# A compressed interaction network: V1 and V0 as packed matmuls of 32 by 64, and another order in the head

## The chip, the cores and the metric

The kernel runs on one core of one Trainium2 chip. A core has TensorE (PE, matmuls from SBUF into PSUM), VectorE (DVE), ScalarE (ACT), GpSimd (POOL) and SyncE (SP, which here only issues DMAs); each works through its own queue in order and waits for others by semaphores. PEld is TensorE's loading of weights. The metric is the time of one execution on the device, in microseconds; lower is better.

## The reference: what is computed

For a batch of B = 1024 with F = 64 fields and E = 16 elements, all in fp32, with `x` of shape (1024, 64, 16):

```python
x0, h, xs = x, x, []
for i in range(3):                                   # W[i]: (128, 64 * 64), b[i]: (128,)
    z = einsum('bfe,bge->bfge', x0, h)               # products of all pairs of rows
    y = einsum('oc,bce->boe', W[i], z.reshape(B, 64 * 64, E)) + b[i][None, :, None]
    if i < 2: x_i, h = y[:, :64], y[:, 64:]          # half goes out, half goes on
    else:     x_i = y
    xs.append(x_i)
out = sum(concatenate(xs, axis=1), axis=2) @ fc_w.T + fc_b      # (1024, 1)
```

## The kernel before

**The algebra.** Only a weighted sum of the outputs is wanted. So the last layer's weights are first contracted with fc (v2t, 64 numbers for each half), and then with the second layer's (a matrix M, written to DRAM as `md` and read back mirrored as `ms`). The outputs of layers 0 and 1 that go out directly come to quadratic forms in x (V0) and in x and h1 (V1), where V0 and V1 are 64x64 matrices: W0 and W1 weighed with fc.

**The chunks.** N = 512 columns (32 batch rows by 16 elements) make one chunk; there are 32 of them. A chunk's x is loaded twice: `xa` (128 rows by 4 tiles; x at shifted rows) and `xb` (4 further shifts), 1 MB each. `product` (line 219) multiplies them on VectorE, four instructions of 128x2048 for a chunk, into 16 tiles z of 128x512. `contract` (line 256) multiplies the 16 tiles by `w_all` on TensorE and adds up in one PSUM tile `acc`: 64 columns of weights make h1, 64 others make q. Of the last group's first tile 32 rows are squares x*x, written by ScalarE (line 228).

**The packed block.** For every 4 chunks `contract_shared` (line 265) adds what is left. V1 times x goes into `acc` (line 274), V0 times x into a PSUM tile `y` for two chunks (line 278): 64x64 matmuls whose operand `xx` holds one chunk's 64 rows of x in the upper half of the partitions and the next chunk's in the lower half. V1 lies twice, one below the other, in `v1w`; V0 lies twice on the diagonal of the 128x128 tile `bd`. The squares of rows 0 to 31 of four chunks lie in the four row groups of one tile `sq`; they are multiplied as 32x64 matmuls (line 284). `xx` and `sq` are filled by ScalarE from `xa`: one copy of 64x512 (line 243) and one square of 32x512 (line 234) for a chunk.

**The head.** Four chunks, HEAD = [2, 3, 0, 1], are worked on before M is known. For the first two, `xb` isn't loaded but shifted out of `xa` by matmuls with a shift matrix (`shift_pair`, line 180, into PSUM tiles xp). `half_contract` (line 291) contracts only h1 for them; `keep_h1` saves it in SBUF. Between the four, TensorE makes v2t (line 411) and M (line 435, tiles pm); ScalarE copies pm to `m_sb` (line 445); six DMAs write it to `md` (lines 460 to 470, on the queues of SP and ScalarE), more read it back (lines 497 and 503), and VectorE adds it up as weights (`q_weights`, line 533). Then `head_q` (line 314) contracts q for the kept chunks, and the normal chunks follow in the order 4, 5, 6, 7, 2, 3, 8, 9, ... (line 618), chunks 2 and 3 standing for both kept pairs' turns. V1 is weighed after the products of chunk 4 (lines 576 to 582), V0 after those of chunk 5 (line 586 on).

**What sets the order.** The schedule is written out by hand: on each engine instructions run in the order in which the program issues them. DMAs on SP's queue are issued in that order too, so one that waits for its buffer holds up those behind it. Tiles come from pools with a fixed number of buffers (`bufs`); a tile that is asked for anew waits for the last use of the one whose place it takes.

**Start.** Six matmuls with `bd` (set to zero by GpSimd; `keep_clock(6)`, line 107) run before x has landed, another one after the first shifts, and then two matmuls for the constant `cst` (line 198).

## Time and profile before

| | |
|---|---|
| median of 3 runs | 486.74 us (486.42 to 490.46) |
| the profiled execution | 486.68 us, its span 484.9 us |
| instructions in the trace | 4057 |
| TensorE busy | 479.8 us (99%) |
| VectorE busy | 370.4 us (76%) |
| ScalarE busy | 93.8 us (19%) |
| GpSimd busy | 17.3 us (4%) |
| SP's DMA queue | 77.05 MB, 41.4% of 16 engines' span |
| `contract`, line 260 | 928 records, 387.3 us |
| V1, line 274 / V0, line 278 | 66 / 64 records, 15.5 us each |
| squares, line 284 | 132 records, 8.9 us and more (two forms) |
| ScalarE's copies to xx, line 243 | 32, 0.613 us each |
| ScalarE's squares to sq, line 234 | 32, 0.628 us each |

The span runs from the first to the last instruction in the profile; the execution's own time is 1.8 us longer. "Busy" counts the time in which at least one instruction of an engine ran, so matmuls that run side by side in different parts of the array count once. The chain that ended last is followed back from the end, at each step to what released it. In a timeline's line stand the start in us, the length in us, engine, line of the kernel, operation, output and inputs, shape and count, and in brackets the idle time before it with what ended it. Every fp32 matmul leaves two records.

### The profile page before, as it was taken

How to read it: one execution, taken by the hardware profiler on the slowest of the kernel's cores; microseconds unless marked ns; L12 is line 12 of the kernel's file. 1: busy time of each engine (PE TensorE's matmuls, PEld its weight loads, DVE VectorE, ACT ScalarE, POOL GpSimd, SP SyncE). 2: the span in 40 equal slices, each digit the busy share in tenths (PEclk: the TensorE clock that was granted, in tenths of full speed). 3: DMA queues.
4: the chain of work that ended last, by engine and by line, in shares of the span. 5: the costliest groups of instructions: out<-in, count | busy, mean ns of one | idle time of the engine just before them, and what ended most of it. 6: DMA issues, size and time to landing. Idle time of an engine off the chain costs nothing.

```text
span 484.9 us, 4057 instructions
## 1 busy us (share of the span) xinstructions
PE 479.8 (99%) x1672; PEld 215.7 (44%) x1672; DVE 370.4 (76%) x234; ACT 93.8 (19%) x165; POOL 17.3 (4%) x15
## 2 busy tenths in 40 slices
PE   9999999999999999999999999999999999999996
PEld 4564344443344344444444344443444434444465
DVE  5984799998899988898887686767878676771312
ACT  4244012021212030312221012212022121020001
POOL 5350000000000000000000000000000000000000
PEclk9999999999999999999999999999999999999999
DMA  8986984441743453547343344433344430000000
GB/s 334 412 266 181 427 349 174 173 173 64 307 182 142 173 207 140 194 174 279 113 187 120 148 174 173 161 128 105 126 173 173 170 145 32 0 1 0 0 2 0
DMA packets 14392, 78.59 MB, mean 162 GB/s; under 512 B 3778, under 2 KB 4450, under 8 KB 5478
## 3 DMA queue, kind: packets, MB, share of 16 engines
q1 hardware_dynamic: 13266, 77.05, 41.4%
q10 hardware_dynamic: 1108, 1.28, 1.0%
q8 instruction: 13, 0.21, 0.2%
q14 instruction: 5, 0.04, 0.0%
HBM read 76.69 MB, written 1.64 MB: 162 GB/s over the span
## 4 chain that ended last, share of the span: by engine, by line
PE 97%; DVE 1%; ACT 1%; SPq 1%; issue 1%; DMA 0%; POOL 0%; DVEq 0%; POOLq 0%
PE acc L260 80%; PE acc L314 6%; PE acc L296 4%; PE acc L274 3%; PE acc L284 2%; PE xp L184 1%; PE misc L105 1%; SPq L465 0%; DVE z L223 0%; ACT m_sb L445 0%; PE pv L411 0%; DMA md<-m_sb 0%; PE pm L435 0%; PE y L278 0%; PE po L604 0%
## 5 line engine op out<-in xcount | busy, mean ns | idle before, releaser
L260 PE MATMUL acc<-z,w_all 128*128 128x512 f32 (+1 forms) x928 | 387.3, 578 | 0.0
L223 DVE TENSOR_TENSOR z<-xa,xb 128x2048 f32<-128x2048 f32 x125 | 280.7, 2286 | 41.4 <-PE acc L260 34.8
L260 PEld LDWEIGHTS acc<-z,w_all 128*128 128x128 f32 x928 | 175.5, 190 | 211.3 <-issue 205.8
L228 ACT ACTIVATE z<-xa 32x512 f32<-32x512 f32 x34 | 21.3, 626 | 322.7 <-DVE z L223 318.1
L336 DVE SCALAR_TENSOR_TENSOR uu<-acc,vs,q 64x512 f32<-64x512 f32 (+1 forms) x29 | 21.2, 731 | 57.7 <-ACT q L330 57.5
L296 PE MATMUL acc<-z,w_all 128*64 128x256 f32 x256 | 28.9, 381 | 0.2 <-DVE z L223 0.2
L314 PE MATMUL acc<-z,w_all 128*64 128x512 f32 x128 | 27.9, 593 | 0.0
L330 ACT COPY q<-acc 64x512 f32<-64x512 f32 (+1 forms) x33 | 18.7, 567 | 37.4 <-PE acc L260 21.2
L223 DVE TENSOR_TENSOR z<-xa,xp 128x2048 f32<-128x2048 f32 (+2 forms) x10 | 18.1, 1856 | 7.2 <-PE xp L184 6.0
L296 PEld LDWEIGHTS acc<-z,w_all 128*64 128x64 f32 x256 | 18.0, 137 | 11.0 <-issue 1.3
L234 ACT ACTIVATE sq<-xa 32x512 f32<-32x512 f32 x32 | 20.1, 628 | 3.4 <-DMA xa<-in_xra 2.7
L345 DVE TENSOR_REDUCE acc<-uu 128x64 f32<-128x1024 f32 (+3 forms) x19 | 20.3, 1073 | 0.3
L243 ACT COPY xx<-xa 64x512 f32<-64x512 f32 x32 | 19.6, 613 | 0.3
L314 PEld LDWEIGHTS acc<-z,w_all 128*64 128x64 f32 x128 | 9.1, 137 | 18.0 <-issue 17.9
L278 PE MATMUL y<-xx,bd 64*64 64x512 f32 x64 | 15.5, 603 | 0.0
L274 PE MATMUL acc<-xx,v1w 64*64 64x512 f32 (+1 forms) x66 | 15.5, 588 | 0.0
L341 DVE SCALAR_TENSOR_TENSOR uu<-y,cx,xx 128x512 f32<-128x512 f32 x16 | 11.3, 746 | 0.2
L223 POOL TENSOR_TENSOR z<-xa,xb_gps 128x2048 f32<-128x2048 f32 x2 | 9.1, 4568 | 4.7 <-ACT xb_gps L361 4.4
L284 PE MATMUL acc<-sq,w_sq 32*64 32x512 f32 (+1 forms) x132 | 8.9, 599 | 0.0
L274 PEld LDWEIGHTS acc<-xx,v1w 64*64 64x64 f32 x66 | 4.1, 132 | 10.6 <-issue 10.3
L223 POOL TENSOR_TENSOR z<-xa,xb 128x2048 f32<-128x2048 f32 x1 | 6.6, 6570 | 13.3 <-DVE z L223 13.3
L184 PE MATMUL xp<-xa,shift 64*64 64x512 f32 x32 | 5.5, 786 | 0.1
(57 smaller groups left out, 60.0 us busy)
## 6 DMA issues: line engine op xcount, KB each, us to landing
xa<-in_xra SPq DMA_DIRECT2D x32, 1024.0 KB, 5.0
xb<-in_xrb SPq DMA_DIRECT2D x31, 1024.0 KB, 7.1
w<-in_w2t SPq DMA_DIRECT2D x2, 1024.0 KB, 10.9
xa<-in_xra SPq DMA_DIRECT2D x2, 768.0 KB, 7.9
w1s<-in_w1h SPq DMA_DIRECT2D x1, 1024.0 KB
w1x<-in_wx SPq DMA_DIRECT2D x1, 1024.0 KB
w0x<-in_wx SPq DMA_DIRECT2D x1, 1024.0 KB, 8.3
w0t<-in_w0r SPq DMA_DIRECT2D x1, 768.0 KB
```

The costliest lines, as they stand in the source:

```text
L223: engine.tensor_tensor(zs[c, j][:, at, :], xas[c][:, at, :], xbs[c][j].unsqueeze(1).to_broadcast([128, last - first, N]), ALU.mult,)
L228: nc.scalar.activation(zs[c, j][SQ, 0, :], xas[c][SQ, 0, :], AF.Square)
L234: nc.scalar.activation(sqs[c // 4][at], xas[c][0:32, 0, :], AF.Square)
L243: nc.scalar.copy(xxs[c // 2][to], xas[c][to, 0, :])
L260: nc.tensor.matmul(acc_c, w_all[:, t, w_cols(c)], zs[c, j][:, i, cols], start=(t == 0 and c % 4 < 2), stop=(t == NT - NI and c % 4 >= 2),)
L274: nc.tensor.matmul(acc_c[q], v1w[rows], xxs[k][rows, cols], start=(c not in ends), stop=False,)
L284: nc.tensor.matmul(acc_c[halves[n]], w_sq[at, w_cols(c)][:, 64 * n : 64 * n + 64], sqs[first // 4][at, cols], start=h and (first == 0 or c ...
L296: nc.tensor.matmul(accs[c][halves[n]], w_all[:, t, 0:64], zs[c, j][:, i, n * H2 : (n + 1) * H2], start=(t == 0), stop=(j == last and i == ...
L314: nc.tensor.matmul(accs[c][halves[1 - c % 2]], w_all[:, t, 64:128], zs[c, j][:, i, :], start=(t == 0), stop=False,)
L330: nc.scalar.copy(q[h, cols], acc_c[64 - h.start : 128 - h.start])
L336: nc.vector.scalar_tensor_tensor(uu[:, cols], acc_c[h], bh1[h], q[h, cols], ALU.add, ALU.mult)
L345: nc.vector.tensor_reduce(acc[rows, of, k, half], uus[k][rows, of, E * half.start : E * half.stop].rearrange("p k (b e) -> p k b e", e=E), ...
```

## The change

Five things are changed.

1. **V1 and V0 in 32x64.** `load_shared` (new) loads x for four chunks into `xr`: 128 rows, chunk n's rows 0 to 31 (part 0) and 32 to 63 (part 1) in row group n. `v1w` and `v0w` hold V1 and V0 by row group and part. Each of the four chunks has for each part one V1 and one V0 matmul of 32x64, so 16 in place of 8.
2. **x by DMA.** `load_shared` also loads `xx` (two DMAs of 256 KB, as `xr` has), and one ScalarE instruction squares 128x512 into `sq`. The function `last_tile` with its copies and squares is gone, for the head's chunks too. `load_shared(n)` is issued after chunk n's own load, for n divisible by four; for chunks 0 to 3 ahead of chunk 8's products.
3. **The weights' copies.** `to_groups` copies V1 and V0 in 32x32 pieces, 16 each, where there were 4 copies of 64x32 each.
4. **The start.** The first matmuls take the zeros that the program always has, seven of 128x128 and one of 128x64; `bd` and the later `keep_clock(1)` are gone. The constant's matmuls stand behind the first two tiles of chunk c0's contraction.
5. **The head's order.** Products of c0 on GpSimd and one on VectorE are cut in two; the second pair of c1's shifts comes after `half_contract(c0, 1)`; `half_contract(c1, 0)` comes after v2t; the last x of c2 is copied into PSUM; the third DMA that writes `md` goes from ScalarE's queue to SP's; the copies of c3's x, with cx behind them, come before `keep_h1(c1)`; GpSimd's product of c3 is issued before c2's contraction and contracted second.

The diff, cut to its core (smaller const tiles now share `res` and `shift`):

```diff
-    keep_clock(6)
+    zeros = nc.const_aps.tensor(0.0, [128, 128])
+    for n in (128,) * 7 + (64,):
+        nc.tensor.matmul(misc[:, 0:n], zeros, zeros[:, 0:n], start=True, stop=True)
...
+    def load_shared(first):
+        xr = xrs[first] = sp.tile([128, 2, N], F32, tag="xr", name=f"xr_{first}")
+        for h in range(2):
+            nc.sync.dma_start(
+                out=xr[:, h, :],
+                in_=bass.AP(
+                    tensor=xra.tensor, offset=(first * XR + 32 * h) * N,
+                    ap=[[XR * N, 4], [N, 32], [1, N]],
+                ),
+            )
+        for k in (first // 2, first // 2 + 1):
+            xxs[k] = sp.tile([128, N], F32, tag="xx", name=f"xx_{k}", bufs=4)
+            nc.sync.dma_start(
+                out=xxs[k],
+                in_=bass.AP(
+                    tensor=xra.tensor, offset=2 * k * XR * N, ap=[[XR * N, 2], [N, F], [1, N]]
+                ),
+            )
+        sqs[first] = sp.tile([128, N], F32, tag="sq", name=f"sq_{first}")
+        nc.scalar.activation(sqs[first], xr[:, 0, :], AF.Square)
...
-    keep_clock(1)
-    cst = const_tile("cst", [128, 1])
...
-            for n in range(2):
-                c, rows, q = 2 * k + n, halves[n], halves[1 - n]
+        groups = {c: slice(32 * (c % 4), 32 * (c % 4) + 32) for c in chunks}
+        for m in range(2):
+            for c, at in groups.items():
+                n, xr = c % 2, xrs[first][groups[c], m]
                 for acc_c, cols in pieces(c):
                     nc.tensor.matmul(
-                        acc_c[q], v1w[rows], xxs[k][rows, cols], start=(c not in ends), stop=False,
+                        acc_c[halves[1 - n]], v1w[at, m], xr[:, cols],
+                        start=(m == 0 and c not in ends), stop=False,
+                        tile_position=(at.start, 64 * (1 - n)),
                     )
-            for rows in halves:
-                nc.tensor.matmul(ys[k][rows], bd[rows, rows], xxs[k][rows], start=True, stop=True)
+                nc.tensor.matmul(
+                    ys[c // 2][halves[n]], v0w[at, m], xr, start=(m == 0), stop=(m == 1),
+                    tile_position=(at.start, 64 * n),
+                )
...
-    product(c0, 1, engine=nc.gpsimd)
+    for i in (0, 2):
+        product(c0, 1, i, i + 2, engine=nc.gpsimd)
...
+    half_contract(c0, 0, at=(0, 1))
+
+    cst = const_tile("cst", [128, 1])
...
-    product(c0, 2)
+    product(c0, 2, 0, 2)
     h1_weights(1, w0o[1])
+    product(c0, 2, 2, NI)
...
-    half_contract(c0, 0)
+    half_contract(c0, 0, at=(2, 3))
...
     shift_pair(c1, (0, 3))
+    half_contract(c0, 1)
     shift_pair(c1, (1, 2))
...
-    half_contract(c0, 1, 2, 3, last=3)
+    half_contract(c0, 2, 3, last=3)
...
-    half_contract(c1, 0)
...
-    half_contract(c1, 3, 1)
+    half_contract(c1, 0, 3, 1)
...
+    xb2 = ps.tile([128, N], F32, tag="set", name=f"xp_{c2}_{NJ - 1}")
+    nc.scalar.copy(xb2, xbs[c2][NJ - 1])
+    xbs[c2][NJ - 1] = xb2
...
-    nc.scalar.dma_start(out=m_ap(64, 32, [[row, 32], [1, 32 * F]]), in_=m_rows[64:96])
+    nc.sync.dma_start(out=m_ap(64, 32, [[row, 32], [1, 32 * F]]), in_=m_rows[64:96])
...
-    keep_h1(c1)
-    squares(c2)
-    new_acc(c2, H2)
     for j in (0, 1):
         xb3 = ps.tile([128, N], F32, tag="y", name=f"xp_{c3}_{j}")
         nc.scalar.copy(xb3, xbs[c3][j])
         xbs[c3][j] = xb3
+    nc.scalar.copy(cx, pcx)
+    keep_h1(c1)
+    new_acc(c2, H2)
     for j in range(NJ):
         product(c2, j)
+    product(c3, NJ - 1, engine=nc.gpsimd)
     half_contract(c2, *range(NJ), last=3)
...
-    half_contract(c3, 0, 1, 3, 2, last=2)
+    half_contract(c3, 0, 3, 1, 2, last=2)
...
-    for c in KEPT:
-        last_tile(c)
...
                 load_chunk(n)
-                last_tile(n)
+                if n % 4 == 0:
+                    load_shared(n)
...
+    def to_groups(w, part):
+        for at in range(0, 128, 32):
+            for n in range(2):
+                for m in range(2):
+                    q = 64 * n + 32 * m
+                    nc.vector.tensor_copy(
+                        w[at : at + 32, m, 32 * n : 32 * n + 32], part[q : q + 32]
+                    )
...
                 for n in order[4:6]:
                     load_chunk(n)
-                    last_tile(n)
+                load_shared(0)
```

More of the change, by code (lines that the diff above doesn't have):

```diff
@@ L96, in cin_kernel @@
     nc.scalar.copy(fv2, fc2.to_broadcast([128, 32]))
-    bd = const_tile("bd", [128, 128])
-    nc.gpsimd.memset(bd, 0.0)
+    v0w = const_tile("v0w", [128, 2, F])
+    v1w = const_tile("v1w", [128, 2, F])
     misc = ps.tile([128, N], F32, tag="acc", name="misc", bufs=4)
-    def keep_clock(n):
-        for _ in range(n):
-            nc.tensor.matmul(misc[:, 0:128], bd, bd, start=True, stop=True)
-    keep_clock(6)
+    zeros = nc.const_aps.tensor(0.0, [128, 128])
+    for n in (128,) * 7 + (64,):
+        nc.tensor.matmul(misc[:, 0:n], zeros, zeros[:, 0:n], start=True, stop=True)
     shift = const_tile("shift", [128, 96])
@@ L125, in cin_kernel @@
     w_sq = const_tile("w_sq", [128, 192])
-    v1w = const_tile("v1w", [128, F])
-    xas, xbs, xxs, sqs = {}, {}, {}, {}
+    res = const_tile("res", [128, 128])
+    xas, xbs, xxs, xrs, sqs = {}, {}, {}, {}, {}
     def load_xa(c, at=slice(0, NI)):
@@ L192, in cin_kernel @@
     shift_pair(c0, (2, 3))
-    keep_clock(1)
-    cst = const_tile("cst", [128, 1])
-    for j in range(2):
-        nc.tensor.matmul(
-            misc[:, 0:1], fcol[:, j : j + 1].to_broadcast([128, 128]), bcol[:, j : j + 1],
-            start=(j == 0), stop=(j == 1),
-        )
     acc = const_tile("acc", [128, 2, NCH // 2, CB])
@@ L228, in product @@
             nc.scalar.activation(zs[c, j][SQ, 0, :], xas[c][SQ, 0, :], AF.Square)
-    def squares(c):
-        if c // 4 not in sqs:
-            sqs[c // 4] = xp.tile([128, N], F32, tag="zl", name=f"sq_{c}", bufs=3)
-        at = slice(32 * (c % 4), 32 * (c % 4) + 32)
-        nc.scalar.activation(sqs[c // 4][at], xas[c][0:32, 0, :], AF.Square)
-    def last_tile(c):
-        if c >= FIRST:
-            squares(c)
-        if c % 2 == 0:
-            xxs[c // 2] = sp.tile([128, N], F32, tag="xx", name=f"xx_{c}", bufs=5)
-        to = halves[c % 2]
-        nc.scalar.copy(xxs[c // 2][to], xas[c][to, 0, :])
     def w_cols(c):
@@ L270, in contract_shared @@
             ys[k] = ps.tile([128, N], F32, tag="y", name=f"y_{k}")
-            for n in range(2):
-                c, rows, q = 2 * k + n, halves[n], halves[1 - n]
+        groups = {c: slice(32 * (c % 4), 32 * (c % 4) + 32) for c in chunks}
+        for m in range(2):
+            for c, at in groups.items():
+                n, xr = c % 2, xrs[first][groups[c], m]
                 for acc_c, cols in pieces(c):
                     nc.tensor.matmul(
-                        acc_c[q], v1w[rows], xxs[k][rows, cols], start=(c not in ends), stop=False,
-                    )
-            for rows in halves:
-                nc.tensor.matmul(ys[k][rows], bd[rows, rows], xxs[k][rows], start=True, stop=True)
-        for c in chunks:
-            at = slice(32 * (c % 4), 32 * (c % 4) + 32)
+                        acc_c[halves[1 - n]], v1w[at, m], xr[:, cols],
+                        start=(m == 0 and c not in ends), stop=False,
+                        tile_position=(at.start, 64 * (1 - n)),
+                    )
+                nc.tensor.matmul(
+                    ys[c // 2][halves[n]], v0w[at, m], xr, start=(m == 0), stop=(m == 1),
+                    tile_position=(at.start, 64 * n),
+                )
+        for c, at in groups.items():
             for acc_c, cols in pieces(c):
@@ L285, in contract_shared, with half_contract @@
                         acc_c[halves[n]], w_sq[at, w_cols(c)][:, 64 * n : 64 * n + 64],
-                        sqs[first // 4][at, cols], start=h and (first == 0 or c not in ends),
+                        sqs[first][at, cols], start=h and (first == 0 or c not in ends),
                         stop=(c in ends), tile_position=(at.start, 64 * n),
                     )
-    def half_contract(c, *js, last=None):
+    def half_contract(c, *js, last=None, at=None):
         for j in js:
-            for i in tiles(j):
+            for i in at or tiles(j):
                 t = j * NI + i
@@ L359, in cin_kernel @@
     new_acc(c0, H2)
-    squares(c0)
     nc.scalar.copy(xb_gps[:, 0, :], xbs[c0][1])
     xbs[c0][1] = xb_gps[:, 0, :]
-    product(c0, 1, engine=nc.gpsimd)
+    for i in (0, 2):
+        product(c0, 1, i, i + 2, engine=nc.gpsimd)
     w0p = ps.tile([128, 2, NI, F], F32, tag="set", name="w0p")
@@ L371, in cin_kernel @@
     product(c0, 0, 2, NI)
+    half_contract(c0, 0, at=(0, 1))
+    cst = const_tile("cst", [128, 1])
+    for j in range(2):
+        nc.tensor.matmul(
+            misc[:, 0:1], fcol[:, j : j + 1].to_broadcast([128, 128]), bcol[:, j : j + 1],
+            start=(j == 0), stop=(j == 1),
+        )
     nc.scalar.activation(cst, misc[:, 0:1], AF.Identity, bias=fcb, scale=float(E))
     nc.scalar.copy(w0o[1], w0s[1][:, :, 1, :])
-    product(c0, 2)
+    product(c0, 2, 0, 2)
     h1_weights(1, w0o[1])
+    product(c0, 2, 2, NI)
     for j in (2, 3):
@@ L390, in cin_kernel @@
     xbs[c1][3] = xb_gps[:, 1, :]
-    squares(c1)
     product(c0, 3)
     load_chunk(c3)
-    half_contract(c0, 1, 2, 3, last=3)
+    half_contract(c0, 2, 3, last=3)
     keep_h1(c0)
@@ L401, in cin_kernel @@
     product(c1, NJ - 1, engine=nc.gpsimd)
-    half_contract(c1, 0)
     v2r = flat_tile("v2r")[:, 0:1024].rearrange("p (n c) -> p n c", n=2)
-    v2t = const_tile("v2t", [128, F])
+    v2t = res[:, 0:F]
     for n in range(2):
-        pv = ps.tile([128, 512], F32, tag=("y", "set")[n], name=f"pv2_{n}")
+        pv = ps.tile([128, 512], F32, tag=("set", "y")[n], name=f"pv2_{n}")
         for k in range(4):
@@ L443, in cin_kernel @@
         nc.tensor.matmul(pcx[to], v2t[0:64], bh2, start=True, stop=True)
+    xb2 = ps.tile([128, N], F32, tag="set", name=f"xp_{c2}_{NJ - 1}")
+    nc.scalar.copy(xb2, xbs[c2][NJ - 1])
+    xbs[c2][NJ - 1] = xb2
     for m in (0, 2, 1, 3):
         nc.scalar.copy(m_sb[:, m, :], pms[m])
-    nc.scalar.copy(cx, pcx)
     half_contract(c1, 2, last=2)
@@ L516, in cin_kernel @@
     new_acc(c3, H2)
-    product(c3, NJ - 1, engine=nc.gpsimd)
     for j in range(NJ - 1):
         product(c3, j)
-    squares(c3)
     keep_h1(c2)
-    half_contract(c3, 0, 1, 3, 2, last=2)
+    half_contract(c3, 0, 3, 1, 2, last=2)
     for j in range(1, NJ):
@@ L526, in cin_kernel @@
             read_columns(j, nc.scalar if half and j == 2 else nc.sync, half)
-    dg = const_tile("dg", [128, F])
+    dg = res[:, F:128]
     nc.sync.dma_start(out=dg[SQ], in_=m_ap(32, 32, [[row + F, 32], [1, F]]))
@@ L571, in weigh @@
         nc.vector.tensor_reduce(out, w, AX.X, ALU.add)
+    def to_groups(w, part):
[5 more added lines that the diff above has]
+                        w[at : at + 32, m, 32 * n : 32 * n + 32], part[q : q + 32]
+                    )
     load_products(FIRST)
@@ L577, in cin_kernel @@
     nc.sync.dma_start(out=w1x, in_=wx1)
-    v1h = const_tile("v1h", [128, 32])
+    v1h = shift[:, 0:32]
     weigh(w1x, fcr[:, 64:128], v1h)
-    for to in halves:
-        for n in range(2):
-            nc.vector.tensor_copy(v1w[to, 32 * n : 32 * n + 32], v1h[halves[n]])
+    to_groups(v1w, v1h)
     load_products(FIRST + 1)
@@ L588, in v0_weights @@
         nc.sync.dma_start(out=w0x, in_=wx0)
-        v0h = const_tile("v0h", [128, 32])
+        v0h = shift[:, 32:64]
         weigh(w0x, fcr[:, 0:64], v0h)
-        for to in halves:
-            for n in range(2):
-                cols = slice(to.start + 32 * n, to.start + 32 * n + 32)
-                nc.vector.tensor_copy(bd[to, cols], v0h[halves[n]])
+        to_groups(v0w, v0h)
     NP = NCH // 2
     QP = NP // 4
-    res = const_tile("res", [128, QP, CB])
+    res = res.rearrange("p (k b) -> p k b", b=CB)
     outs = out.rearrange("(k h b) o -> h k (b o)", h=2, b=CB)
```

## The prediction

> **What bounds the kernel now.** I read the page's busy shares first, then the chain that ended last, then the timelines of single engines where the diff touches them.

> ```profile
> PE 479.8 (99%) x1672; PEld 215.7 (44%) x1672; DVE 370.4 (76%) x234; ACT 93.8 (19%) x165; POOL 17.3 (4%) x15
> ...
> PE 97%; DVE 1%; ACT 1%; SPq 1%; issue 1%; DMA 0%; POOL 0%; DVEq 0%; POOLq 0%
> ```

> TensorE works for 479.8 of 484.9 us and carries 97% of the chain. So an edit counts where it shortens or stops TensorE; VectorE counts only where TensorE catches up with it, ScalarE hardly at all. The profiled execution took 486.68 us, 1.8 us more than its span; the median of the runs shown, 486.74, lies 0.06 us off. I add to 486.68. A change under 1% of this (4.9 us) is about what a measurement of this kernel cannot tell from none: its three runs lie between 486.42 and 490.46.

> **The packed block (V1, V0, squares).** It runs 8 times, once for 4 chunks. This is TensorE's timeline of one (columns: start, us, then engine, line, operation, count):

> ```profile
> 217.25 0.65 PE L274 MATMUL acc<-xx,v1w 64*64 64x512 f32 x2
> 217.26 0.65 PE L278 MATMUL y<-xx,bd 64*64 64x512 f32 x2
> 217.73 0.60 PE L274 MATMUL acc<-xx,v1w 64*64 64x512 f32 x2
> 217.74 0.60 PE L278 MATMUL y<-xx,bd 64*64 64x512 f32 x2
> 218.16 0.60 PE L274 MATMUL acc<-xx,v1w 64*64 64x512 f32 x2
> ...
> 218.58 0.60 PE L274 MATMUL acc<-xx,v1w 64*64 64x512 f32 x2
> ...
> 219.12 1.11 PE L284 MATMUL acc<-sq,w_sq 32*64 32x512 f32 x16
> 220.17 0.70 PE L260 MATMUL acc<-z,w_all 128*128 128x512 f32 x1
> ```

> Each fp32 matmul leaves two records. Four 64x64 matmuls start within 20 ns and the next four 0.43 us later, so four quarters of the array work at once: 16 records in 4 rounds. The 16 records of the squares (32x64) take 1.05 us to the next line's start, two rounds of eight at once. The change makes V1 and V0 into 16 matmuls of 32x64, 32 records. On eight tiles that is again 4 rounds of 0.43: **the matmul time is the same**, since half the height means twice as many. What goes is one change of tile shape: from 218.58 to 219.12 is 0.54 instead of 0.43, and a first round after a change takes 0.48 instead of 0.43; together 0.11 + 0.05 = 0.16 us. Times 8 that is **-1.3 us**. Bounds: that, and nothing if eight tiles writing six accumulators cost as much as the switch did.

> [...]

> **The copies of V1 and V0.** The new weights lie in four row groups and two parts: to_groups copies 16 pieces where 4 were copied (lines 582 and 594 of before). VectorE's timeline between the first normal chunk and the first packed block:

> ```profile
> 51.76 8.90 DVE L223 TENSOR_TENSOR z<-xa,xb 128x2048 f32<-128x2048 f32 x4 [6.08 <-DMA xb<-in_xrb]
> 60.57 2.28 DVE L570 TENSOR_TENSOR w1x<-w1x,vs 128x2048 f32<-128x2048 f32 x1
> 62.89 2.29 DVE L571 TENSOR_REDUCE v1h<-w1x 128x32 f32<-128x2048 f32 x1
> 65.21 0.74 DVE L582 COPY v1w<-v1h 64x32 f32<-64x32 f32 x4
> 65.98 8.90 DVE L223 TENSOR_TENSOR z<-xa,xb 128x2048 f32<-128x2048 f32 x4
> 74.80 2.29 DVE L570 TENSOR_TENSOR w0x<-w0x,vs 128x2048 f32<-128x2048 f32 x1
> 77.12 2.29 DVE L571 TENSOR_REDUCE v0h<-w0x 128x32 f32<-128x2048 f32 x1
> 79.44 0.76 DVE L594 COPY bd<-v0h 64x32 f32<-64x32 f32 x4
> ```

> There is no gap after 51.76: VectorE runs at its limit here. A copy costs 0.187 us (0.74 / 4, starts 0.187 apart); 12 more for each weight are 2.25 us, **4.5 us for both**. The row is 64x32, the new copies 32x32: the same width, so the same time. TensorE starts chunk 5 at 56.47 + 13.8 = 70.3 and needs its first product, ready at 68.3: slack 2.0 us. It starts the packed block at 84.14 and needs V0, ready at 80.2: slack 3.9 us. So the slack is used up: V0 comes at 84.7 even if nothing else moves. Products 0 to 3 of chunk 6 follow at 86.9 and later, before TensorE asks for them; at 110 to 125 the same delay leaves about 1 us of slack for the kept chunks' last products, and from chunk 8 on VectorE waits for others and has caught up.

> **What moves the start at 51.76.** It waits for the load of chunk 4, which stands on SP behind the mirror of M: copies of pm, writes to md, reads of ms. Call its delay X. Two parts:
> - The head on TensorE. The warm-up no longer waits for a memset (start 0.75 instead of 1.00), but has 16 records of 0.21 instead of 12: it ends near 4.2, while the first shift starts at 4.00 today: +0.2 to +0.4. The constant (L198, four records of 0.11) goes behind two tiles of the first contraction and then costs two shape changes; one keep_clock matmul is gone; the second pair of shifts goes behind half_contract(c0, 1): two more shape changes (0.28), and a wait of 0.27 for the product that holds its buffer is gone. Adding up from the start of the first contraction (7.95 in both, since the shift delay uses up what the constant gave there), the contraction of c0's third product starts at 14.4 instead of 13.8: +0.6, and pm with it. If the clock were full earlier (the first shift rounds take 0.86, later ones 0.43), two rounds would save up to 0.86. So -0.3 to +0.6; I take 0.5.
> - The writes. SP's queue now:

> ```profile
> 27.76 0.53 SPq L461 DMA_DIRECT2D md<-m_sb  x1
> 28.34 2.40 SPq L465 DMA_DIRECT2D md<-m_sb  x1
> 30.78 2.25 SPq L466 DMA_DIRECT2D md<-m_sb  x1
> 33.07 1.53 SPq L467 DMA_DIRECT2D md<-m_sb  x1
> 36.71 0.47 SPq L503 DMA_DIRECT2D ms<-md  x1
> ```

> L464 (256 KB), issued by ScalarE at 28.36 for 2.35 us, becomes SP's second. If a slow issue is only the wait for the bytes being written, which stay the same, it costs 0; if it costs its row again, all behind it comes 2.4 us later. Earlier is excluded, as the last write is issued from the same queue, one place later. I take the middle, 1.1, since both queues' second issues ended at the same 30.7, which looks like a shared limit. Everything behind on SP moves along: 10 reads or loads up to chunk 4.

> So X = 0.5 + 1.1 = **1.6 us** (bounds -0.3 and 3.0). The reads of ms have room: the weights of j = 0 come at 40.5 + 1.6, TensorE wants them at 42.64 + 0.4; those of j = 1 at 44.3 + 1.6 against 46.4. With the writes at their upper bound j = 1 would be late by some 0.5 us, which lies within the wait below and adds nothing to it.

> **The sum.** V0 is ready at 84.7 + 1.6 = 86.3 instead of TensorE's 84.14: the packed block starts 2.1 us late (about 1.3 us of it already at chunk 5's first product). From there TensorE is alone again, and 8 blocks give back 1.3: +0.8, **487.5 us**.

> **At nothing:**
> - ScalarE loses 32 copies (0.61) and the squares of 32x512 (0.63), gains 8 squares of 128x512 and one copy of c2's last x: it is busy 19%, and TensorE's work hides it. Without that cover it would be a gain of some 35 us.
> - load_shared adds 32 loads of 256 KB, 8 on 78.6 MB, where the DMA engines are busy 41%. Its place hurts only behind chunk 4, ahead of w1x: at some 400 GB/s, 2.5 to 3.5 us later for w1x and chunk 5. Both have room (loaded near 57 and 62 + X, wanted at 60.6 and 68 + X); without it that stall would be VectorE's.
> - ScalarE's x copies for c3 come before its hb work: VectorE's 1.22 us of waiting there goes, and TensorE's wait of 0.16 at 37.4. What is late next is POOL's product of c3, ended at 36.1 today and now wanted at 38.

> **Rivals.**
> - *VectorE keeps up* (X near 0, copies hidden): only the 1.3 comes off, with the head's 0.4 back: 485.8. For it: 2.0 and 3.9 us of slack. Against: 4.5 us of copies.
> - *The mirror takes the place of the gain* (slower side). One queue issues all writes but one, X reaches 3.0 or more, TensorE stands still ahead of the first packed block: 86.3 + 1.4 and more, so 489 to 490. It decides from X = 0.7 on, where it equals the gain; from X = 5.6 on the kernel would be over 1% slower.
> - *The tiles do not pack.* If only four 32x64 tiles ran at once, V1 and V0 would take 8 rounds: +1.7 x 8 = 13.7, 500 us. The squares' rows speak against it.
> - *The change does not do what it says:* a packed block still of 2.9 us; then 488.8.

> **Chances.** Forecast (487.0 to 488.3) 0.42; VectorE keeps up or nearly (485.3 to 487.0) 0.2; mirror late (488.3 to 490) 0.22, beyond 490 to 491.5 0.06; block not shorter 0.05, its time within these; tiles not packing or X over 5.6 0.05. The range 485.3 to 489.9 holds a little over 0.8. Faster by over 1%: 0.02, as no case reaches 481.8; slower by over 1%: 0.06; the rest 0.92.

> **What would show it.** The packed block 2.76 us from its first matmul to the next L260-like line, with no gap ahead of the squares; 16 copies of 3.0 us ahead of V1 and V0; VectorE's chunk 4 starting near 53.4; TensorE idle near 70 and 86 us, 2 us in all, "waiting for DVE". Wrong if that idle time is missing or over 4 us, if a round of eight tiles takes over 0.45, or if the head's contraction starts much off 8.0.

## The result, and the profile after

| | before | after |
|---|---|---|
| median of the comparison (6 runs each) | 486.72 us (486.42 to 490.66) | **503.29 us** (503.06 to 503.75) |
| ratio after / before, 95% interval | | **1.0317** (1.0277 to 1.0356) |
| the profiled execution, its span | 486.68, 484.9 us | 503.75, 501.4 us |
| mean granted clock of TensorE (1 is full speed) | 1.000 | 0.986 |

The change costs 16.6 us; the forecast was 487.5 us with a range that ended at 489.9. Single executions of before and of some variants below lie 3 to 5 us above their medians, so some ratios below have wide intervals and lie off the quotient of the medians.

The page of after, its busy shares, its chain that ended last, and one of its costliest groups:

```profile
PE 480.9 (96%) x1804; PEld 218.8 (44%) x1804; DVE 374.0 (75%) x259; ACT 60.3 (12%) x110; POOL 15.5 (3%) x15
...
PE 75%; DMA 14%; DVE 6%; SPq 3%; issue 1%; ACT 1%; DVEq 0%
...
L581 DVE TENSOR_TENSOR w1x<-w1x,vs 128x2048 f32<-128x2048 f32 x1 | 2.3, 2293 | 11.6 <-DMA w1x<-in_wx 11.6
```

TensorE is busy for 1.1 us more than before, not 16, but it carries 75% of the chain instead of 97%, and DMA 14% instead of 0. The third line names the place: one instruction of VectorE, the weighing of w1x, waited 11.6 us for its load. TensorE's timeline of after (start, length, ..., in brackets the idle time before and what ended it):

```profile
56.58 14.00 PE L259 MATMUL acc<-z,w_all 128*128 128x512 f32 x32
83.04 16.22 PE L259 MATMUL acc<-z,w_all 128*128 128x512 f32 x32 [12.46 <-DVE z L237]
99.19 0.64 PE L275 MATMUL acc<-xr,v1w 32*64 32x512 f32 x1
99.19 0.64 PE L280 MATMUL y<-xr,v0w 32*64 32x512 f32 x1
...
99.67 0.59 PE L275 MATMUL acc<-xr,v1w 32*64 32x512 f32 x1
...
100.10 0.59 PE L275 MATMUL acc<-xr,v1w 32*64 32x512 f32 x1
...
100.53 0.59 PE L275 MATMUL acc<-xr,v1w 32*64 32x512 f32 x1
...
100.96 1.06 PE L288 MATMUL acc<-sq,w_sq 32*64 32x512 f32 x16
101.95 27.73 PE L259 MATMUL acc<-z,w_all 128*128 128x512 f32 x64
...
160.91 13.97 PE L259 MATMUL acc<-z,w_all 128*128 128x512 f32 x32 [0.65 <-DVE z L237]
...
179.20 3.27 PE L259 MATMUL acc<-z,w_all 128*128 128x512 f32 x7 [1.56 <-DVE z L237]
```

Chunk 4 starts 0.1 us later than before (56.47). Then TensorE waits 12.5 us for chunk 5's first product, and chunk 5 takes 16.15 us to the next line instead of 13.8: 2.3 more. The packed block is 2.76 us (99.19 to 101.95). Chunks 9 and 10 wait another 0.65 and 1.56. The eight blocks give back 8 x 0.16 = 1.3. The sum is 0.1 + 12.5 + 2.3 + 2.2 - 1.3 = 15.8 of the 16.5 us by which the span grew; 0.7 is not assigned. VectorE's timeline of after in the same stretch:

```profile
52.53 8.90 DVE L237 TENSOR_TENSOR z<-xa,xb 128x2048 f32<-128x2048 f32 x4 [6.56 <-DMA xb<-in_xrb]
73.05 2.29 DVE L581 TENSOR_TENSOR w1x<-w1x,vs 128x2048 f32<-128x2048 f32 x1 [11.62 <-DMA w1x<-in_wx]
75.38 2.29 DVE L582 TENSOR_REDUCE shift<-w1x 128x32 f32<-128x2048 f32 x1
77.70 2.97 DVE L590 COPY v1w<-shift 32x32 f32<-32x32 f32 x16
80.70 8.90 DVE L237 TENSOR_TENSOR z<-xa,xb 128x2048 f32<-128x2048 f32 x4
```

The weighing stands in VectorE's queue ahead of chunk 5's products, so these wait with it. Before, it started at 60.57 with no wait. Next, SP's queue of after, which issues the loads:

```profile
45.17 0.40 SPq L135 DMA_DIRECT2D xa<-in_xra  x1
45.62 0.43 SPq L148 DMA_DIRECT2D xb<-in_xrb  x1
46.09 1.19 SPq L155 DMA_DIRECT2D xr<-in_xra  x2
47.32 6.55 SPq L164 DMA_DIRECT2D xx<-in_xra  x2
53.97 3.47 SPq L598 DMA_DIRECT2D w1x<-in_wx  x1
```

The two DMAs for xx hold SP for 6.55 us, where the 1 MB load of xa took 0.40 (what this holding costs is taken up with e1 and e9). And four stretches of the span of after (stretch; its us; busy us and records of PE, PEld, DVE, ACT, POOL; granted clock; mean busy share of the 16 DMA engines; GB/s):

```profile
47.00:51.00 4.00, 4.00 (x22) 1.39 (x20) 0.00 (x0) 0.00 (x0) 0.00 (x0) 1.00 0.99 399
53.00:57.00 4.00, 4.00 (x19) 1.30 (x16) 4.00 (x3) 0.63 (x1) 0.00 (x0) 1.00 0.27 102
59.00:69.00 10.00, 10.00 (x24) 4.40 (x24) 2.43 (x2) 0.63 (x1) 0.00 (x0) 1.00 1.02 313
136.00:142.00 6.00, 6.00 (x30) 2.02 (x28) 4.70 (x4) 1.84 (x3) 0.00 (x0) 1.00 0.13 51
```

While chunk 4's x comes in, the engines move 399 GB/s. Then, with xr and xx on the way, 102 GB/s at a share of 0.27, which is 4.3 engines of 16; at 136 to 142 us, when the loads for chunks 0 to 3 are coming in, xx last, 51 GB/s at 0.13, which is 2.1 engines. The source of xr is written as [chunk 4][row 32][column], that of xx as [chunk 2][row 64][column]: the outermost sizes are 4 and 2. That is the theory which the runs below test: **a load whose source has an outermost size of 4 or 2 runs on about as many DMA engines (4.3 and 2.1 of 16 by these shares), at 102 and 51 GB/s; it holds up the loads behind it, w1x first, in the issuing queue or on those engines; VectorE waits, TensorE waits, and behind TensorE's wait of 12.46 us its granted clock is 0.50, from 73.9 to 87.5 us.** Rivals: the 8 MB and 32 DMAs more, whatever their form; the rest of the change (head, copies, tiles); the place of the loads alone.

### The profile page after: what moved, and what is told of

Read it like the earlier page. It is cut to its first block, busy times and chain, and to the rows that moved or that the text cites. A ratio compares the mean times of both kernels' runs of the same rounds, so it can differ in the third digit from the quotient of the medians.

```text
span 501.4 us, 4369 instructions
## 1 busy us (share of the span) xinstructions
PE 480.9 (96%) x1804; PEld 218.8 (44%) x1804; DVE 374.0 (75%) x259; ACT 60.3 (12%) x110; POOL 15.5 (3%) x15
## 3 DMA queue, kind: packets, MB, share of 16 engines
q10 hardware_dynamic: 1060, 1.02, 0.8%
## 4 chain that ended last, share of the span: by engine, by line
PE 75%; DMA 14%; DVE 6%; SPq 3%; issue 1%; ACT 1%; DVEq 0%
PE acc L259 68%; DMA xb<-in_xrb 4%; DMA w1x<-in_wx 4%; DMA xr<-in_xra 3%; DVE z L237 3%; PE acc L300 3%; PE acc L275 2%; DMA md<-m_sb 1%; DMA w0t<-in_wh 1%; PE acc L288 1%; SPq L135 1%; SPq L511 1%; DVE uu L338 1%; DVE hb L337 1%; DVE v1w L590 1%
## 5 line engine op out<-in xcount | busy, mean ns | idle before, releaser
L237 DVE TENSOR_TENSOR z<-xa,xb 128x2048 f32<-128x2048 f32 x124 | 277.7, 2285 | 42.0 <-PE acc L259 27.5
L237 DVE TENSOR_TENSOR z<-xa,xp 128x2048 f32<-128x2048 f32 (+2 forms) x12 | 20.4, 1748 | 6.1 <-PE xp L207 6.1
L334 ACT COPY q<-acc 64x512 f32<-64x512 f32 (+1 forms) x33 | 18.7, 566 | 37.4 <-PE acc L259 21.4
L280 PE MATMUL y<-xr,v0w 32*64 32x512 f32 x128 | 15.9, 601 | 0.0
L275 PE MATMUL acc<-xr,v1w 32*64 32x512 f32 (+1 forms) x132 | 15.7, 587 | 0.0
L581 DVE TENSOR_TENSOR w1x<-w1x,vs 128x2048 f32<-128x2048 f32 x1 | 2.3, 2293 | 11.6 <-DMA w1x<-in_wx 11.6
L237 POOL TENSOR_TENSOR z<-xa,xb_gps 128x1024 f32<-128x1024 f32 (+1 forms) x3 | 9.3, 3104 | 5.4 <-ACT xb_gps L364 4.6
L275 PEld LDWEIGHTS acc<-xr,v1w 32*64 32x64 f32 x132 | 5.1, 131 | 9.9 <-issue 9.6
L171 ACT ACTIVATE sq<-xr 128x512 f32<-128x512 f32 x8 | 5.0, 630 | 12.1 <-DMA xr<-in_xra 12.0
L237 POOL TENSOR_TENSOR z<-xa,xb 128x2048 f32<-128x2048 f32 x1 | 4.8, 4832 | 12.5 <-DMA xb<-in_xrb 12.5
```

Of the source, the lines that this page charges most:

```text
L237: engine.tensor_tensor(zs[c, j][:, at, :], xas[c][:, at, :], xbs[c][j].unsqueeze(1).to_broadcast([128, last - first, N]), ALU.mult,)
L275: nc.tensor.matmul(acc_c[halves[1 - n]], v1w[at, m], xr[:, cols], start=(m == 0 and c not in ends), stop=False, tile_position=(at.start, 6 ...
L280: nc.tensor.matmul(ys[c // 2][halves[n]], v0w[at, m], xr, start=(m == 0), stop=(m == 1), tile_position=(at.start, 64 * n),)
L334: nc.scalar.copy(q[h, cols], acc_c[64 - h.start : 128 - h.start])
```

## The experiments

### e1_spread: the same loads, by chunk

```diff
-        for h in range(2):
+        for c in range(first, first + 4):
             nc.sync.dma_start(
-                out=xr[:, h, :],
-                ... offset=(first * XR + 32 * h) * N, ap=[[XR * N, 4], [N, 32], [1, N]],
+                out=xr[32 * (c % 4) : 32 * (c % 4) + 32],
+                ... offset=c * XR * N, ap=[[N, 32], [32 * N, 2], [1, N]]
...
-            nc.sync.dma_start(
-                out=xxs[k],
-                ... offset=2 * k * XR * N, ap=[[XR * N, 2], [N, F], [1, N]]
+            for h in range(2):
+                nc.sync.dma_start(
+                    out=xxs[k][halves[h]],
+                    ... offset=(2 * k + h) * XR * N, ap=[[N, F], [1, N]]
```

> The changed kernel, but load_shared issues x by chunk: four DMAs of 128 KB for xr (32 rows each) and four for xx (64 rows each), instead of two and two whose outermost dimension is 4 or 2. Same bytes, same 2 KB packets, same place in SP's queue. Theory (the old form runs on 4 and 2 of the 16 DMA engines, and w1x and chunk 5, spread over all 16, wait for those few): w1x lands before 61 us, TensorE's wait of 12.5 us near 70 and the half clock after it go, likewise the waits near 160 and 177; left are the 4.5 us of copies against 3.9 us of slack, the late start of 0.8 us and the 1.3 us of the packed blocks: 486.5 to 488.5 us. Rival (1 MB more in 2 KB packets is what delays w1x, however it is spread): 498 to 503 us.

Measured: 486.57 us (before in the same comparison 486.64), ratio 0.9982 (0.9954 to 1.001). The whole loss is gone, with the same bytes and with twice as many DMAs. VectorE's timeline of this kernel, and below it SP's queue:

```profile
51.92 8.90 DVE L237 TENSOR_TENSOR z<-xa,xb 128x2048 f32<-128x2048 f32 x4 [6.59 <-DMA xb<-in_xrb]
60.74 2.28 DVE L581 TENSOR_TENSOR w1x<-w1x,vs 128x2048 f32<-128x2048 f32 x1
...
65.38 2.97 DVE L590 COPY v1w<-shift 32x32 f32<-32x32 f32 x16
68.38 8.90 DVE L237 TENSOR_TENSOR z<-xa,xb 128x2048 f32<-128x2048 f32 x4
```

```profile
47.23 5.05 SPq L164 DMA_DIRECT2D xx<-in_xra  x4
52.51 0.40 SPq L598 DMA_DIRECT2D w1x<-in_wx  x1
```

The weighing no longer waits. Yet SP is held for 5.05 us by xx here too, and w1x's issue ends at 52.91 instead of 57.44: of the 12 us by which w1x was late in after, the issue explains at most 4.5, and the rest arose behind it. Chunk 5's products come at 68.38 plus one product's time, so TensorE waits a little:

```profile
70.72 14.00 PE L259 MATMUL acc<-z,w_all 128*128 128x512 f32 x32 [0.78 <-DVE z L237]
```

These 0.78 us are the forecast's late VectorE, at a smaller size; e5 below prices it.

### e2_dead_slow and e3_dead_spread: only the loads, in the kernel before

Both add to the kernel before the loads of `load_shared`, into tiles that nothing reads, at the same places of SP's queue (some small tiles share their places, and the pools of xx and sq have one buffer less, for room): e2 in the change's form, e3 by chunk as in e1.

```diff
+    def load_dead(first):
+        xr = sp.tile([128, 2, N], F32, tag="xr", ...)
...
                 load_chunk(n)
+                if n % 4 == 0:
+                    load_dead(n)
```

> The kernel before, with the changed kernel's loads for xr and xx added in their old form and place, into tiles that nothing reads; small tiles share space as in the changed kernel. Nothing else of the change. Theory (the loads alone do it): w1x lands near 73 us, TensorE waits some 10 us before chunk 5, runs at half clock after that, waits again near 160: 498 to 503 us. Rival (the loads hurt only together with the late mirror and the longer copies): 487 to 491 us.

> The same as the kernel with dead loads in the old form, but these loads issued by chunk as eight DMAs of 128 KB. Theory (few engines): no wait of TensorE is added, 486.4 to 487.5 us. Rival (bytes and packets): as with the old form, 498 to 503 us.

Measured: e2 497.58 us, ratio 1.0209 (1.0147 to 1.0272); e3 486.60 us, ratio 1.0013 (0.9971 to 1.0056). VectorE's timeline of e2, and then TensorE's:

```profile
71.71 2.29 DVE L592 TENSOR_TENSOR w1x<-w1x,vs 128x2048 f32<-128x2048 f32 x1 [11.29 <-DMA w1x<-in_wx]
```

```profile
79.48 15.49 PE L279 MATMUL acc<-z,w_all 128*128 128x512 f32 x32 [9.19 <-DVE z L242]
```

So no other part of the change is needed for most of the loss: the loads alone make w1x wait 11.29 us and cost 10.9 us. That falls a little short of what was expected, and e2 stays 5.7 us under after. Of that, 12.46 - 9.19 = 3.3 us is TensorE's shorter wait: in e2 there are 12 copies fewer between w1x and chunk 5's products (12 x 0.187 = 2.2 us), and w1x is there 1.3 us earlier. The rest was not taken apart. e3 shows that 8 MB more cost nothing.

### e4_later: the loads behind chunk n+1's

```diff
-                if n % 4 == 0:
-                    load_shared(n)
+                if n % 4 == 1:
+                    load_shared(n - 1)
```

> The changed kernel with load_shared(n) issued behind chunk n+1's load instead of ahead of it, in its old form on few engines; so w1x and chunk 5 stand ahead of it, w0x and chunk 6 behind. Theory (whatever stands behind the slow loads is late by some 15 us): the wait before chunk 5 goes, a smaller one appears before the packed block or chunk 6, as w0x is wanted at 78 and chunk 6 at 86: 488 to 496 us. Rival (the total of DMA work counts, not the place): unchanged, 500 to 504 us.

Measured: 488.90 us, ratio 1.0027 (0.9996 to 1.0058). The slow loads stay; now w1x and chunk 5's x are ahead of them, and w0x behind. VectorE's timeline of e4:

```profile
79.94 2.29 DVE L581 TENSOR_TENSOR w0x<-w0x,vs 128x2048 f32<-128x2048 f32 x1 [2.12 <-DMA w0x<-in_wx]
```

w0x is 2.12 us late and the copies of V0 end at 87.6, so the first packed block takes 4.97 us (85.21 to 90.18) instead of 2.76, and chunk 5 waits 0.60. What these loads cost depends on what is queued behind them: 488.90 us here, 503.29 in after.

### e8_xx_slow and e9_xr_slow: one of the two in the old form

e8 is after with e1's loads for xr and the old ones for xx (outermost size 2); e9 the other way round (outermost size 4).

> The changed kernel with xr spread by chunk and xx in its old form (outermost dimension 2, seen at some 50 KB per us). Theory (each form's cost is its bytes at its own pace: xr 5.2 us, xx 10.4 us of the 15.6 us, 1.3 us each when spread): w1x some 4 us earlier than in the changed kernel, near 69 us, TensorE's wait before chunk 5 some 8 to 9 us: 494 to 499 us. Rival (the pace is that of 2 KB packets, the form of the loads doesn't matter): no difference to the changed kernel, 503 us.

> The changed kernel with xx spread and xr in its old form (outermost dimension 4, seen at some 100 KB per us). Theory as above: w1x near 64 us, TensorE's wait some 3 to 4 us, no half clock: 487.5 to 491 us. Rival (one slow form is as bad as both, since what follows waits for the slowest engine): 494 us and more.

Measured: e8 497.51 us, ratio 1.0228 (1.0207 to 1.0248); e9 494.08 us, ratio 1.0157 (1.0137 to 1.0177). VectorE's line for w1x in e8, and then in e9:

```profile
69.99 2.29 DVE L580 TENSOR_TENSOR w1x<-w1x,vs 128x2048 f32<-128x2048 f32 x1 [7.55 <-DMA w1x<-in_wx]
```

```profile
66.08 2.29 DVE L582 TENSOR_TENSOR w1x<-w1x,vs 128x2048 f32<-128x2048 f32 x1 [4.78 <-DMA w1x<-in_wx]
```

Size 2 delays w1x more than size 4, and both together most (11.62). e8 is as expected. e9 came out above: w1x came later than thought, and behind TensorE's wait of 5.88 us chunk 5 took 16.09 us, where chunk 4 took 14.00; the mean granted clock of the profiled execution is 0.991 (before 1.000). Its time lies in the rival's range, but the rival itself does not hold: one slow form is 9.2 us better than both. SP's queue of e9 shows that the holding of SP is not needed for the delay:

```profile
50.28 0.53 SPq L599 DMA_DIRECT2D w1x<-in_wx  x1
```

w1x is issued 2.2 us earlier than in e1, and is used at 66.08, 15.8 us after its issue began; in e1 it was there within 8.2 us (60.74, with no wait). It is late as a transfer.

Against e1 the two cost 10.9 and 7.5 us, after 16.7; they do not add up. The longer chunk 5 behind the wait is one reason: 2.2 to 2.7 us in each of the three; in after the granted clock is 0.50 for the first 4.5 us of it.

### e10_warm: TensorE kept at work in the wait

Fourteen matmuls by zeros (0.86 us each) into an unused tile before chunk 5.

```diff
+        if s == 1:
+            warm = ps.tile([128, N], F32, tag="y", name="warm")
+            for _ in range(14):
+                nc.tensor.matmul(
+                    warm, zeros, hb[:, 0, :], start=True, stop=True
+                )
         if not head:
```

> The changed kernel with 14 matmuls of zero weights by a 128x512 tile (0.86 us each, 12.0 us) ahead of chunk 5's contraction, their result unused; they stand where TensorE waited 12.5 us. Theory (the half clock after the wait is the idle time's doing and costs 2.3 us on top of it): the granted clock stays full, chunk 5 takes 13.8 instead of 16.2 us: 500.5 to 501.5 us. Rival (the half clock has another cause): 503 us and more.

Measured: 503.61 us, ratio 1.0356 (1.0339 to 1.0373); after has 503.29. TensorE's timeline of e10:

```profile
69.89 12.18 PE L658 MATMUL warm<-hb,const-float32-0.0 128*128 128x512 f32 x28
82.38 14.00 PE L259 MATMUL acc<-z,w_all 128*128 128x512 f32 x32 [0.32 <-DVE z L237]
```

Chunk 5 takes 14.0 us again, at a granted clock of 1.00 from 72 to 90 us, so the 16.2 was the clock, and here the idle time was the clock's cause. But the time is the same, where 500.5 to 501.5 was expected. Chunk 6 starts 2.9 us earlier than in after (99.08), and then meets the second group's slow loads:

```profile
160.04 5.37 PE L259 MATMUL acc<-z,w_all 128*128 128x512 f32 x8 [2.65 <-DVE z L237]
```

Chunk 9 starts only 0.9 us earlier than in after, having waited 2.65 us instead of 0.65, and the clock falls there: the stretch from 160 to 164 us has a granted clock of 0.57. That fall belongs to this execution (502.92 us, mean granted clock 0.995); the three others have 0.997 to 1.000 and are no faster. In the trace, most of a gain ahead of a late transfer is lost at that transfer; where the other executions lose it is not shown.

### e11_outer: the same DMAs, dimensions exchanged

```diff
-                    ap=[[XR * N, 4], [N, 32], [1, N]],
+                    ap=[[N, 32], [XR * N, 4], [1, N]],
...
-                    ... ap=[[XR * N, 2], [N, F], [1, N]]
+                    ... ap=[[N, F], [XR * N, 2], [1, N]]
```

Number of DMAs, bytes and length of a row stay; only the outermost size of the source is 32 and 64 instead of 4 and 2. The rows land in another order, so V1's, V0's and the squares' parts are computed from permuted rows; every instruction has the same shape.

> The changed kernel with the two outer dimensions of each load's source pattern exchanged: [32 rows][4 chunks][512] for xr, [64 rows][2 chunks][512] for xx. As many DMAs, as many bytes and 2 KB rows as in the changed kernel, in the same place; rows of x land in other partitions than the weights expect, so V1's, V0's and the squares' shares of the output are those of permuted rows. Theory (the outermost dimension of the pattern decides over how many of the 16 DMA engines one DMA is spread): 32 and 64 rows spread over all, 486 to 488 us as with loads by chunk. Rival (what helped was that more, smaller DMAs ran side by side): 500 us and more.

Measured: 486.91 us, ratio 1.0004 (0.9987 to 1.0021). SP's queue of e11:

```profile
45.81 1.27 SPq L155 DMA_DIRECT2D xr<-in_xra  x2
47.13 1.27 SPq L164 DMA_DIRECT2D xx<-in_xra  x2
48.50 0.54 SPq L598 DMA_DIRECT2D w1x<-in_wx  x1
```

A stretch of e11 after chunk 4's loads (columns as above):

```profile
51.00:54.00 3.00, 3.00 (x16) 1.00 (x14) 1.67 (x1) 0.63 (x1) 0.00 (x0) 1.00 1.02 396
```

396 GB/s at a share of 1.02, and xx holds SP for 1.27 us instead of 6.55. VectorE weighs w1x at 61.15 with no wait. Not the number of DMAs, not the bytes, not the place: **here the outermost size decides**, 396 GB/s at 32 and 64 against after's 102 and 51 at 4 and 2. (The exchange also changes the order in which rows are read from DRAM, which no run separates; that after's loads kept only 4.3 and 2.1 engines busy, by the shares, speaks for the spread.)

### e5_act_copies: e1 with the copies on ScalarE

```diff
-                    nc.vector.tensor_copy(
+                    nc.scalar.copy(
                         w[at : at + 32, m, 32 * n : 32 * n + 32], part[q : q + 32]
```

> The kernel with the loads spread by chunk (486.57 us), and the 32 copies of V1 and V0 into row groups on ScalarE instead of VectorE. Theory (what kept that kernel from a gain is the 6 us of copies on VectorE, which leave TensorE waiting 0.8 us before chunk 5 and about 0.7 us before the first packed block): both waits go, the 1.3 us of eight shorter packed blocks are left: 484.6 to 485.5 us, ratio to before about 0.997. Rival (the waits come from the late load of chunk 4, not from the copies): 486.3 to 486.8 us.

Measured: 485.30 us (before 486.58), ratio 0.9979 (0.9969 to 0.9989). VectorE's timeline has nothing between V1's reduction and chunk 5's products, and TensorE (second fence) goes from chunk 4 through chunk 5 without a gap:

```profile
66.09 8.89 DVE L237 TENSOR_TENSOR z<-xa,xb 128x2048 f32<-128x2048 f32 x4
```

```profile
56.34 27.73 PE L259 MATMUL acc<-z,w_all 128*128 128x512 f32 x64
```

The copies' price in e1 was thus 486.57 - 485.30 = 1.3 us, and the shorter blocks bring 1.3. The wait of 0.7 us before the first packed block, of which the expectation speaks, is not in e1's trace: that block takes 2.78 us (84.65 to 87.43), and only about 0.9 of the 1.3 us shows.

### e7_head_only: the kernel before with only the start and the head's order

> The start and the head's order alone on the kernel before: warm-up with zeros, constant and shifts moved, halved products, the third write of M on SP, c3's copies first; V1 and V0, the copies and squares of ScalarE and the loads stay as before. Theory (the head's shapes and order move pm by under 1 us and cover is left everywhere): 486.3 to 487.2 us. Rival (the write on SP's queue delays the mirror by up to 2.4 us): the first products of chunk 4 start at 53.5 us or later; the time stays below 488 us.

The edit is parts 4 and 5 of the change, with the old `last_tile`, V1 and V0. Measured: 486.75 us (before 486.58), ratio 1.0001 (0.9985 to 1.0017). Chunk 4's products start at 52.46 (51.76 before), its contraction at 56.28 (56.47 before). The head's order does nothing to the time that these runs could show.

### e6_block_only and e12_block_again: the packed block with the old head

This is e5 with the start and the head of the kernel before: loads by chunk, 32x64 matmuls, copies on ScalarE. e12 is the same kernel again.

```diff
-    zeros = nc.const_aps.tensor(0.0, [128, 128])
...
+    keep_clock(6)
...
-    for i in (0, 2):
-        product(c0, 1, i, i + 2, engine=nc.gpsimd)
+    product(c0, 1, engine=nc.gpsimd)
...
-    nc.sync.dma_start(out=m_ap(64, 32, [[row, 32], [1, 32 * F]]), in_=m_rows[64:96])
+    nc.scalar.dma_start(out=m_ap(64, 32, [[row, 32], [1, 32 * F]]), in_=m_rows[64:96])
```

> The packed block alone on the kernel before: 32x64 matmuls, x by spread loads, copies on ScalarE; the start and the head's order stay as before (the head's squares and copies are gone, as in the change). Theory (the packed block gives 8 x 0.16 us and the head's new order nothing that can be seen): 485.0 to 485.7 us. Rival (the new order of the head is what makes room for it): 486.3 us and more.

> The packed block alone on the kernel before, with spread loads and copies on ScalarE, run once more for a tighter interval (485.18 us so far): 485.0 to 485.5 us, ratio 0.996 to 0.998; if the 1.3 us were chance, the interval takes in 1.

Measured: e6 485.18 us, ratio 0.9996 (0.9968 to 1.0025); e12 485.08 us (before 486.56), ratio 0.9968 (0.9943 to 0.9994). The medians lie 1.4 and 1.5 us under before, as 8 x 0.16 = 1.3 asks. With either head, then, the packed block with spread loads and with its copies off VectorE is slightly faster than both kernels.

## Why the prediction was wrong, by its own steps

- **The failed step is load_shared, under "At nothing".** It costed the 1 MB that stands ahead of w1x "at some 400 GB/s, 2.5 to 3.5 us later for w1x and chunk 5", and found room for it. That price was the author's estimate; chunk 4's loads do move 399 GB/s, at a share of 0.99. The loads went at 102 and 51 GB/s, w1x was weighed at 73.05 instead of 60.57, and TensorE stood still for 12.5 us. e11, with the same DMAs and another outermost size, takes 486.91 us. At the pace assumed the step was right: e3 has those bytes at no cost, and in e1 w1x has no wait. The sentence "without it that stall would be VectorE's" named the mechanism, but no rival carried it and no bound was taken from a slower pace.
- **Left out: the clock.** The working counted a wait as the time of the wait. The wait of 12.5 us cost 2.3 more in the chunk behind it, at a granted clock of 0.50 until 87.5 us. Taken away alone, in e10, this gained nothing in the time.
- **Left out: the next groups.** The loads were thought of at chunk 4 only; chunks 9 and 10 lost another 2.2 us.
- **Packed block: right.** 2.92 to 2.76 us, eight tiles at once in rounds of 0.43. V0's tiles of two row groups write the two halves of one y, start within 0.05 us of each other, and their rounds take 0.43. e5, e6 and e12 show the 1.3 us in the time.
- **Copies: right.** 2.97 and 3.04 us against 3.0. In e1, where the loads were fast, they cost 1.3 us by e5; the forecast had 2.1 us of late V0, with an X that was too large. (By its own terms chunk 5's first product would have been 1.8 us late, 68.3 + 2.25 + 1.6 - 70.3, and not "about 1.3"; the sum does not use that figure.)
- **X: below the forecast.** 52.53 - 51.76 = 0.77 us instead of 1.6 in this pair of traces. The head's 0.5 measured 0.7: m_sb is ready for SP at 28.46 instead of 27.76. One pair does not settle this: chunk 4's products start at 51.5 to 52.2 in before, e2, e3 and e6, which have the old head, and at 51.8 to 53.5 in the nine kernels with the new one; the medians are 0.5 us apart. (e12's trace, of one of its longest executions, is left out.) The write moved to SP, costed at 1.1, cost nothing: SP's queue of after,

```profile
28.46 0.54 SPq L474 DMA_DIRECT2D md<-m_sb  x1
29.04 0.57 SPq L477 DMA_DIRECT2D md<-m_sb  x1
29.66 1.85 SPq L478 DMA_DIRECT2D md<-m_sb  x1
31.55 2.22 SPq L479 DMA_DIRECT2D md<-m_sb  x1
33.82 1.55 SPq L480 DMA_DIRECT2D md<-m_sb  x1
37.41 0.48 SPq L517 DMA_DIRECT2D ms<-md  x1
```

  has five writes where four stood, and yet the first read comes 0.70 us later than before (36.71), as the first write does. This is the lower bound, and it fits the reading that a slow issue is a wait for bytes. The rival "the mirror takes the place of the gain" is not borne out; e7 has it by itself, at no change.
- **What would show it:** the head's contraction starts at 7.96 (8.0 forecast), the third product's at about 14.4 (14.4). "Wrong if that idle time is ... over 4 us" is what happened, at the place named, near 70 us.

With the loads spread by chunk, e1's 486.57 lies 0.9 us under the forecast of 487.5 and inside the outer range, in the case "VectorE keeps up or nearly" and not in the one that was thought likeliest (487.0 to 488.3): X was too large (51.92 - 51.76 = 0.16 us in e1's trace). After takes 16.7 us more than e1, and the form of the loads is all that differs.

## What to carry to other kernels

Before a DMA is costed by the engines' mean rate, look at the outermost size of its pattern: here, at 4 and 2, the loads ran at 102 and 51 GB/s, a quarter and an eighth of the 399 of chunk 4's, and writing the same loads with the rows outermost gave 396. Then ask what stands behind it on the queue that issues it, and who waits for that. A transfer in a slot that "has room" should be given a bound for the case that it is several times slower, and where TensorE would then stand still, for the chunk behind the wait: in after it took 16.22 us instead of 14.00, with a granted clock of 0.50 for its first 4.5 us.

## What the runs showed of the hardware that was not expected

```profile
73.90:83.00 9.10, 0.00 (x0) 0.00 (x0) 8.80 (x20) 0.00 (x0) 0.00 (x0) 0.50 0.85 360
83.00:87.50 4.50, 4.46 (x6) 1.88 (x7) 4.50 (x3) 0.00 (x0) 0.00 (x0) 0.50 0.12 53
```

  The last matmul ended at 70.58; the granted clock fell to 0.50 at 73.9, 3.3 us later, and was back at 1.00 at 87.5, 4.5 us after work began again. In e10 it is 0.57 from 160 to 164 us; for e2, e8 and e9 only the mean of the profiled execution is on record, 0.993, 0.988 and 0.991 (before 1.000). The chunk behind took 1.6 to 2.7 us longer in these five traces, counted to the next line against 13.8; its row lasts 15.67 us in e10 after 2.65 us of waiting, 16.09 in e9 after 5.88, 15.49 in e2 after 9.19, 16.63 in e8 after 9.30 and 16.22 in the changed kernel after 12.46, against 14.00 for chunk 4, so in these five the cost does not grow with the wait. After the waits of 0.65 and 1.56 us in the changed kernel the granted clock is 1.00 (161 to 170 and 180 to 190 us), and e1's chunk 5 took 14.00 after 0.78.
